# A two-layer model on one core: layer 0's experts in blocks of 256 and 128 rows

## The chip, the cores and the metric

The kernel runs on one NeuronCore of a Trainium2 chip. A core has five engines with a queue of instructions each: TensorE (PE, matrix multiplication, results into PSUM), VectorE (DVE), ScalarE (ACT), GpSimd (POOL) and SyncE (SP). DMAs are issued from the queues of SP, ACT and POOL. The metric is the time of one execution in microseconds of device time, the median of several runs. Numbers are float32 throughout, apart from one mask.

## The reference

Two layers work on 32 sequences of 256 tokens with 128 channels, so on T = 8192 tokens. Each layer computes `x = x + s * silu(f)`, where `s` is an attention over the normalized tokens and `f` a mixture of experts over the same tokens:

```
xn = layernorm(x)
s = attention(xn)          # layer 0: causal, (q1 k1 / 8) (q2 k2 / 8) v; layer 1: strided softmax
scores = sigmoid(xn @ gate_w + bias)         # layer 0
top_scores, top_idx = top_k(scores, 2)       # 2 of 8 experts a token
top_scores = top_scores / (sum(top_scores) + 1e-6)
eo = gelu(xn @ up_w[e] + up_b[e]) @ down_w[e] + down_b[e]     # 128 -> 512 -> 128
out = shared(xn) * 0.1 + sum over the two experts of 0.1 * top_score * eo
out = out / (max(abs(out)) + 1e-6)
x = x + s * silu(out)
```

The reference sends each token through all eight experts of layer 0 and weighs the results, of which two count. No token is dropped there, so an expert may have any number of rows, and the sum over the experts is 2T = 16,384 rows. In layer 1 each expert has a capacity of 2048 rows.

## The kernel before, in words

The kernel is written with Tile, a layer that orders the instructions of each engine at compile time, by the order in the program and by when their inputs are ready in its own model, and that sets the semaphores. Instructions put through `inline` keep their order among themselves on their engine.

Layer 0 goes through these stages:

1. `begin` normalizes the tokens and computes the gates' logits. Two steps of attention run beside each part.
2. `route0` (L626) picks two experts for each token, counts, and works out for each of the 16,384 (token, expert) rows its place (`slot0`) in a buffer in DRAM, `disp0`. The rows of an expert lie together and fill whole blocks of TB = 256 rows; the last block of an expert is partly empty. With sizes known only at run time, NB = (2T + 8 x 255) // 256 = 71 blocks are always worked on, whatever the counts. Positions come from matmuls with triangular matrices into two PSUM tiles (`pos`). From the counts (`psn`) a chain of small VectorE instructions makes the number of blocks of each expert (`nb`), their running sum (`ends`), the base of each expert (`base`), the place of each row (`own`, then `slot`), and for each block the rows of the weight table that it needs (`ex0`, then `wrow`). The function yields in between, and three steps of attention are issued at each yield (`RS = 3`).
3. `dispatch` (L697) scatters the 16,384 rows into `disp0`, 128 at a time, in 128 indirect DMAs of POOL. `pace` (L143) sends three and then waits for their landing. A step of attention runs beside four of every five.
4. `experts` (L914) takes the blocks one after the other. `fetch` (L902) gathers the weights of block i + 2 from DRAM into one of three buffers (`wt`, an indirect DMA of POOL, 592 KB), and loads the block's rows (`xd`, from SP). A block is transposed on PE (`xdt`, copied to `xdT` by DVE), multiplied with the up weights (`eup`, two PSUM tiles of 512 columns, so two 128-channel parts of the 512 in each), put through Gelu by ACT into `ha`, and, one block later, multiplied with the down weights (`edn`). DVE adds the bias (`od`), ACT multiplies each row with its gate, and POOL scatters 128 rows at a time to their tokens in `moe0`, at indices (`to`, by `places`, L180) that POOL works out from the row's own number.
5. The rest of the steps of attention run beside `combine0`, which adds up, normalizes and finishes layer 0. Layer 1 follows.

The attention of layer 0 is a generator of 256 steps (`attention0`, 8 for each of 32 sequences). `step` (L1033) issues the next one, with a piece of the shared expert. The main program hands the steps out: 30 beside `begin`, 12 in routing (four yields), 103 in dispatch, 71 beside the experts. `experts` yields after the transposes, after each half of the up-projection and after the down-projection, four times a block, and a step is issued at every fourth yield (`BLOCK = 4`). That makes 216; 40 are left for the combining stage, whose plan counts from there.

What sets the order around the change: PE works through its queue in the compiled order, so a block whose weights have not landed holds up everything behind it. The three `wt` buffers mean that the gather of block i + 2 can start when block i - 1 is done. On POOL the gathers share a queue with the scatters and with `to`, whose four buffers make it wait for earlier scatters. The three PSUM tiles of `mm_tile` are shared by all these stages.

Of the kernel before, what the change touches and what calls it, by code (L numbers as in the profile page):

```python
# [57 lines left out]
def model_kernel(ctx: ExitStack, tc: tile.TileContext, a: dict, out: bass.AP):  # L58
# [17 lines left out]

    NB = (2 * T + E * (TB - 1)) // TB
    disp0 = dram.tile([(2 * T // TB + E) * TB, ROW], F32, name="disp0")
# [205 lines left out]
    def mm_tile(name):  # L284
        return ps_m.tile([P, 512], F32, tag="mm", name=name)
# [256 lines left out]
    with ExitStack() as c0:  # L542
# [83 lines left out]
        def route0():  # L626

            with ExitStack() as cr:
# [7 lines left out]
                NJ = T // TB  # L636
                starts = rp.tile([P, NJ], F32, name="starts")
                nc.gpsimd.iota(starts, [[TB, NJ]], base=0, channel_multiplier=0,
                               allow_small_or_imprecise_dtypes=True)
                more = rp.tile([P, E, NJ], F32, name="more")  # L640
                nc.vector.tensor_tensor(more, bc(psn[:, :E], 2, NJ), bc(starts, 1, E), ALU.is_gt)
                nb = rp.tile([P, E], F32, name="nb")
                nc.vector.tensor_reduce(nb, more, AX.X, ALU.add)
                ends = nb
                for d in (1, 2, 4):
                    e2 = rp.tile([P, E], F32, name=f"ends{d}")
                    nc.vector.tensor_copy(e2[:, :d], ends[:, :d])
                    nc.vector.tensor_tensor(e2[:, d:], ends[:, d:], ends[:, : E - d], ALU.add)
                    ends = e2
                base = rp.tile([P, E], F32, name="base")  # L650
                nc.vector.tensor_tensor(base, ends, nb, ALU.subtract)
                nc.vector.tensor_scalar(base, base, float(TB), -1.0, ALU.mult, ALU.add)
                own = rp.tile([P, E, 2 * NT], F32, tag="totb", name="own")
                for e in range(E):
                    nc.vector.scalar_tensor_tensor(own[:, e, :], pos[e // 4][:, e % 4, : 2 * NT],
                                                   base[:, e : e + 1], ohf[:, e, :], ALU.add, ALU.mult)
                slot = rp.tile([P, 2 * NT], F32, name="slot")
# [4 lines left out]

                blk = rp.tile([P, NB], F32, name="blk")
                nc.gpsimd.iota(blk, [[1, NB]], base=0, channel_multiplier=0,
                               allow_small_or_imprecise_dtypes=True)
                row = rp.tile([P, 1], F32, name="row")
                nc.gpsimd.iota(row, [[0, 1]], base=0, channel_multiplier=1,
                               allow_small_or_imprecise_dtypes=True)
                ex0 = rp.tile([P, NB], F32, name="ex0")
                nc.vector.tensor_scalar(ex0, blk, ends[:, 0:1], None, ALU.is_ge)  # L670
                for e in range(1, E - 1):
                    nc.vector.scalar_tensor_tensor(ex0, blk, ends[:, e : e + 1], ex0, ALU.is_ge, ALU.add)
                nc.vector.tensor_scalar(ex0, ex0, float(P), row, ALU.mult, ALU.add)
# [24 lines left out]
        def dispatch():  # L698
            for k in range(2):
                if k:  # L700
                    nc.gpsimd.tensor_scalar(xr[:, :, P], xr[:, :, P], float(-T), None, ALU.add)
                    nc.gpsimd.tensor_copy(xr[:, :, P + 1], gate0[:, 1, :])
                for n in range(NT):
                    out0.put(slot0[:, k, n : n + 1], xr[:, n, :], NB * TB)
                    yield
# [144 lines left out]
        def attention0():  # L850
# [48 lines left out]
            for _ in tail:  # L899
                pass  # L900

        def fetch(i):  # L902

            wt = ek.tile([P, NW], F32, tag="wt", name="wt", bufs=3)
            nc.gpsimd.indirect_dma_start(
                out=wt, out_offset=None, in_=a["wexp"][:, :],
                in_offset=bass.IndirectOffsetOnAxis(ap=wrow[:, i : i + 1], axis=0),
            )
            xd = ek.tile([P, TB // P, ROW], F32, tag="xd", name="xd", bufs=4)
            get = nc.sync.dma_start(xd, disp0[i * TB : (i + 1) * TB, :].rearrange("(p s) d -> p s d", p=P))  # L910
            out0.behind(get)
            return wt, xd

        def experts():  # L914

            got = {i: fetch(i) for i in range(2)}
            last = None
            for i in range(NB + 1):
                if i < NB:
                    if i + 2 < NB:  # L920
                        got[i + 2] = fetch(i + 2)
                    wt, xd = got.pop(i)
                    pst = mm_tile("xdt")
                    with queued([PE] if i == 0 else []):
                        for s in range(TB // P):
                            nc.tensor.transpose(pst[:, s * P : (s + 1) * P], xd[:, s, :P], ident)
                    xdT = ek.tile([P, TB], F32, tag="xdT", name="xdT")
                    nc.vector.tensor_copy(xdT, pst[:, :TB])
                    yield
                    ha = ek.tile([P, NFC, TB], F32, tag="ha", name="ha", bufs=2)  # L930
                    for h in range(2):
                        psu = mm_tile("eup")
                        for f in (2 * h, 2 * h + 1):
                            pu = psu[:, (f % 2) * TB : (f % 2 + 1) * TB]
                            nc.tensor.matmul(pu, lhsT=wt[:, f * P : (f + 1) * P], rhs=xdT,  # L935
                                             start=True, stop=True)
                        for f in (2 * h, 2 * h + 1):
                            pu = psu[:, (f % 2) * TB : (f % 2 + 1) * TB]
                            b = FF + NFC * P + f
                            nc.scalar.activation(ha[:, f, :], pu, AF.Gelu, bias=wt[:, b : b + 1])  # L940
                        yield
                if last is not None:
                    wl, hl, xl = last
                    tl = places(ek, xl)
                    psd = mm_tile("edn")[:, :TB].rearrange("p (s c) -> p s c", s=TB // P)
                    for s in range(TB // P):
                        for f in range(NFC):
                            nc.tensor.matmul(psd[:, s, :], lhsT=hl[:, f, s * P : (s + 1) * P],  # L948
                                             rhs=wl[:, FF + f * P : FF + (f + 1) * P],
                                             start=(f == 0), stop=(f == NFC - 1))  # L950
                    od = ek.tile([P, TB // P, P], F32, tag="od", name="od")
                    nc.vector.tensor_tensor(od, psd, bc(wl[:, NW - P : NW], 1, TB // P), ALU.add)
                    for s in range(TB // P):
                        nc.scalar.activation(od[:, s, :], od[:, s, :], AF.Copy, scale=xl[:, s, P + 1 : P + 2])  # L954
                        back0.put(tl[:, s : s + 1], od[:, s, :], 2 * T, order=at_once)
# [129 lines left out]
        for n, _ in enumerate(experts()):  # L1085
            if n % BLOCK == 0:
                step()
# [272 lines left out]
```

## Time and profile before

| what | us |
|---|---|
| time, median of 3 runs | 1929.27 (1926.44 to 1931.02) |
| the profiled execution: its own time | 1932.48 |
| its span, first to last instruction | 1930.6 |
| PE busy (matmuls) | 1805.7, 94% of the span |
| DVE, ACT, POOL busy | 1175.4, 962.0, 847.5 |
| routing, 142 to 190 | 48: PE busy 46.8, DVE 46.2 |
| dispatch, 190 to 452 | 262: PE busy 258.3, DVE 181.0, POOL 137.7 |
| experts, 452 to 938 | 486: PE busy 472.8, ACT 232.7, POOL 226.7, DVE 184.0 |
| combining, 938 to 1153 | 215: PE busy 179.7, DVE 161.5 |
| layer 1, from 1153 | 778 |

Times are counted from the first instruction of the profiled execution. Busy time is the union of an engine's instructions. PEld is the loading of weights into the array, which lies beside the matmuls. One matmul of float32 shows as two records. In a line of the timeline the columns are start, length, engine, line of the kernel, operation, what is written and read, and the number of instructions merged into the line; in square brackets is how long the engine was idle before it, and what ended the wait. In a line of a group the columns behind the bars are the busy time, the mean length of one record in ns, and the idle time before them with what ended it.

### The profile page before, as it was taken

What the parts mean: (1) busy time and instruction counts of PE and PEld (TensorE: products, weight loads), DVE (VectorE), ACT (ScalarE), POOL (GpSimd) and SP (SyncE); (2) the same over time, 40 slices, a digit from 0 to 9 for tenths busy, and PEclk for the clock granted to TensorE, in tenths of its full rate; (3) what the DMA queues carried; (4) which work ended last, traced back from release to release, by engine and by line L of the source; (5) the groups of instructions that cost most, each with busy time, mean ns of one, the idle gap of its engine ahead of it and who ended that gap; (6) DMA issues with size and microseconds to landing.
All of it is one profiled execution on the core that took longest, in us unless ns stands there. A gap on an engine that the chain in (4) does not pass through costs nothing.

```text
span 1930.6 us, 45909 instructions
## 1 busy us (share of the span) xinstructions
PE 1805.7 (94%) x18616; PEld 1394.5 (72%) x18616; DVE 1175.4 (61%) x2227; ACT 962.0 (50%) x2180; POOL 847.5 (44%) x991
## 2 busy tenths in 40 slices
PE   5999999998999999999887799999999799999997
PEld 4777777776888888887765676677777577777765
DVE  6659667665333433443577597888888433335786
ACT  5433333334444544545354575577677333335776
POOL 3001555543444544444545540044544355555454
PEclk8999999999999999999988777999999899999998
DMA  8911211112344443434334410211111122222343
GB/s 279 385 52 31 69 56 43 45 44 67 126 137 125 138 142 125 134 125 137 116 105 143 137 50 7 71 67 34 32 34 33 51 73 67 72 69 84 90 113 101
DMA packets 127524, 183.86 MB, mean 95 GB/s; under 512 B 16340, under 2 KB 83183, under 8 KB 127312
## 3 DMA queue, kind: packets, MB, share of 16 engines
q1 hardware_dynamic: 96096, 92.45, 16.2%
q0 software_dynamic: 28336, 79.73, 12.3%
q10 hardware_dynamic: 2880, 8.74, 1.2%
q8 instruction: 147, 2.41, 0.5%
q14 instruction: 65, 0.53, 0.1%
HBM read 104.11 MB, written 78.00 MB: 94 GB/s over the span
## 4 chain that ended last, share of the span: by engine, by line
PE 31%; ACT 8%; DVE 5%; DMA 2%; issue 2%; POOL 2%; SPq 1%; ACTq 0%; DVEq 0%; POOLq 0%
PE mpsu L1186 6%; PE mpsd L1200 6%; PE apsc L378 3%; PE apsT L406 3%; PE apav L415 3%; ACT apT L408 3%; ACT apr L398 2%; PE apsk L338 2%; PE apsc L384 2%; DMA rows<-moe 1%; PE apsq L350 1%; PE apsv L358 1%; PE mpst L1179 1%; DVE apr L396 1%; DMA soin<-part 1%
## 5 line engine op out<-in xcount | busy, mean ns | idle before, releaser
L166 POOL DMA_INDIRECT moe<-od,to x270 | 270.0, 1000 | 124.3 <-issue 70.8
L777 ACT COPY qk<-ptr 128x512 f32<-128x512 f32 x256 | 138.2, 588 | 241.9 <-PE ptr L775 241.4
L792 DVE TENSOR_TENSOR pat<-pp,dmask 128x1024 f32<-128x1024 f32 x128 | 156.2, 1221 | 109.6 <-PE pp L790 109.6
L395 DVE TENSOR_REDUCE amx<-apsc 128x4 f32<-128x496 f32 x256 | 170.2, 665 | 38.6 <-PE apsc L384 38.5
L408 ACT COPY apT<-apsT 124x512 f32<-124x512 f32 x256 | 142.8, 584 | 100.8 <-PE apsT L406 99.9
L790 PE MATMUL pp<-qk 64*128 64x128 f32 x2048 | 172.6, 297 | 15.8 <-DVE pat L792 14.1
L790 PEld LDWEIGHTS pp<-qk 64*128 64x128 f32 x2048 | 136.8, 194 | 58.4 <-issue 42.5
L396 DVE TENSOR_TENSOR apr<-apsc,amx 128x496 f32<-128x496 f32 x256 | 172.4, 673 | 9.1
L940 ACT ACTIVATE ha<-eup,wt 128x256 f32<-128x256 f32 x284 | 119.0, 471 | 111.8 <-PE eup L935 57.7
L935 PE MATMUL eup<-xdT,wt 128*128 128x256 f32 x568 | 150.2, 390 | 10.8 <-ACT od L954 7.1
L166 POOL DMA_INDIRECT disp<-xr,slot x128 | 132.4, 1034 | 62.7 <-issue 26.7
L744 DVE TENSOR_TENSOR feat<-rot 128x1024 f32<-128x1024 f32 x128 | 157.5, 1272 | 3.9
L406 PE MATMUL apsT<-ident,apr 128*124 128x128 f32 x1024 | 150.7, 293 | 8.3 <-ACT apr L398 3.5
L775 PE MATMUL ptr<-ident,feat 128*128 128x128 f32 x1024 | 146.9, 288 | 7.6 <-DVE feat L744 7.6
L166 POOL DMA_INDIRECT disp<-xr,sidx x128 | 126.7, 990 | 55.0 <-issue 24.7
L415 PE MATMUL apav<-ava,apT 124*64 124x9 f32 x4096 | 143.4, 205 | 0.0
L415 PEld LDWEIGHTS apav<-ava,apT 124*64 124x64 f32 x4096 | 136.8, 140 | 8.8 <-issue 8.4
L948 PEld LDWEIGHTS edn<-wt,ha 128*128 128x128 f32 x1136 | 137.8, 192 | 3.6
L948 PE MATMUL edn<-wt,ha 128*128 128x128 f32 x1136 | 138.1, 275 | 0.0
L775 PEld LDWEIGHTS ptr<-ident,feat 128*128 128x128 f32 x1024 | 114.7, 145 | 29.9 <-issue 13.9
L406 PEld LDWEIGHTS apsT<-ident,apr 128*124 128x124 f32 x1024 | 120.9, 148 | 16.2 <-ACT apr L398 8.8
L935 PEld LDWEIGHTS eup<-xdT,wt 128*128 128x128 f32 x568 | 99.5, 190 | 45.0 <-issue 27.4
(250 smaller groups left out, 3342.8 us busy)
## 6 DMA issues: line engine op xcount, KB each, us to landing
disp<-zero SPq DMA_DIRECT2D x17, 1040.0 KB, 8.5
rows<-moe SPq DMA_DIRECT2D x64, 256.0 KB, 3.9
xd<-disp SPq DMA_DIRECT2D x71, 130.0 KB, 2.3
xd<-disp SPq DMA_DIRECT2D x32, 260.0 KB, 2.8
x<-in_x SPq DMA_DIRECT2D x32, 256.0 KB, 4.6
moe<-zero SPq DMA_DIRECT2D x8, 1024.0 KB, 14.4
part<-so ACTq DMA_DIRECT2D x16, 512.0 KB, 3.5
soin<-part SPq DMA_DIRECT2D x16, 512.0 KB, 4.7
```

The costliest lines, as they stand in the source:

```text
L166: ins = order(lambda: nc.gpsimd.indirect_dma_start(out=self.dst[:, :], out_offset=bass.IndirectOffsetOnAxis(ap=idx, axis=0), in_=rows, in_ ...
L395: inline(nc.vector.tensor_reduce(mx, sv, AX.X, ALU.max))
L396: inline(nc.vector.tensor_tensor(to, sv, bc(mx, 2, NK), ALU.subtract))
L406: nc.tensor.transpose(psT[:NK, j, :], pr[:, 4 * g + j, :], ident)
L408: inline(nc.scalar.copy(pT[:NK], psT[:NK]))
L415: nc.tensor.matmul(avv[u * QB : (u + 1) * QB, h, :], lhsT=pT[:NK, j, u * QB : (u + 1) * QB], rhs=va[:NK, 2 * st + u, h, :], start=True, st ...
L744: inline(eng.tensor_tensor(f[:, n].rearrange("p (h i j) -> p h i j", i=D, j=D), bc(r[:, n], 3, D), bc(r[:, 2 + n], 2, D), ALU.mult))
L775: inline(nc.tensor.transpose(pst[:, 2 * n + c], seq.feat[c][:, n, m * P : (m + 1) * P], ident))
L790: inline(nc.tensor.matmul(pp[:, w, i, c], lhsT=qk[r, 2 + c], rhs=qk[r, c], start=True, stop=True))
L792: inline(nc.vector.tensor_tensor(pat.rearrange("p w i c q -> p (w i c) q"), pp.rearrange("p w i c q -> p (w i c) q"), bc(dmask, 1, 8), ALU ...
L935: nc.tensor.matmul(pu, lhsT=wt[:, f * P : (f + 1) * P], rhs=xdT, start=True, stop=True)
L948: nc.tensor.matmul(psd[:, s, :], lhsT=hl[:, f, s * P : (s + 1) * P], rhs=wl[:, FF + f * P : FF + (f + 1) * P], start=(f == 0), stop=(f == ...
```

## The change

Layer 0's blocks get two sizes. Of each expert's rows, as many blocks of 256 are taken as can be filled with more than 128 rows in the last one; a rest of 1 to 128 rows gets a block of 128. All the blocks of 256 lie first in `disp0`, the small ones behind. There are always 60 places of 256 rows and 15 of 128 (units of 128 rows: 135, where it were 142); where the experts need more than 60 whole blocks, the others are worked on as two small ones each. The blocks are taken in turns: four of 256, then one of 128.

- `route0` counts for both sizes: tiles of twice the width, `shift` and `full` for the rows that go to small blocks, two instructions for each expert on `own` where it was one, and one product over all of it. The table of the blocks' experts takes 15 instructions on `ex0` where it took 7.
- `route0` yields once more, in the middle of `own`, so three more steps of attention are issued in routing.
- A small block has one transpose, one PSUM tile of 4 x 128 columns for the up-projection, Gelus of 128 columns, half the down-projection and one scatter of rows. It yields three times where a whole block yields four times: 285 yields in all.
- No step of attention is issued before the 16th yield of the experts. With one at every fourth from there, 68 steps run beside the experts where it were 71. The sum before combining stays 216.

```diff
-    NB = (2 * T + E * (TB - 1)) // TB
+    HB = TB // 2
+    WHOLE = (2 * T // HB - E) // 2
+    NU = (2 * T + E * (HB - 1)) // HB
+    NB = NU - WHOLE
...
-                starts = rp.tile([P, NJ], F32, name="starts")
+                starts = rp.tile([P, 2, NJ], F32, name="starts")
...
-                more = rp.tile([P, E, NJ], F32, name="more")
-                nc.vector.tensor_tensor(more, bc(psn[:, :E], 2, NJ), bc(starts, 1, E), ALU.is_gt)
-                nb = rp.tile([P, E], F32, name="nb")
-                nc.vector.tensor_reduce(nb, more, AX.X, ALU.add)
+                more = rp.tile([P, E, 2 * NT], F32, tag="totb", name="more")[:, :, : 2 * NJ]
+                nc.vector.tensor_tensor(more, bc(psn[:, :E], 2, 2 * NJ),
+                                        bc(starts.rearrange("p k j -> p (k j)"), 1, E), ALU.is_gt)
+                begun = rp.tile([P, E, 2], F32, name="begun")
+                nc.vector.tensor_reduce(begun, more.rearrange("p e (k j) -> p e k j", k=2), AX.X, ALU.add)
+                nb = rp.tile([P, 2, E], F32, name="nb")
+                nc.vector.tensor_copy(nb[:, 0, :], begun[:, :, 1])
+                nc.vector.tensor_tensor(nb[:, 1, :], begun[:, :, 0], begun[:, :, 1], ALU.subtract)
...
+                shift = rp.tile([P, E], F32, name="shift")
+                nc.vector.tensor_scalar(shift, ends[:, 0, :], ends[:, 0, E - 1 :], -float(TB), ALU.subtract, ALU.mult)
+                nc.vector.scalar_tensor_tensor(shift, base[:, 1, :], float(HB), shift, ALU.mult, ALU.add)
+                full = rp.tile([P, E], F32, name="full")
+                nc.vector.tensor_scalar(full, nb[:, 0, :], float(TB), None, ALU.mult)
...
                 for e in range(E):
-                    nc.vector.scalar_tensor_tensor(own[:, e, :], pos[e // 4][:, e % 4, : 2 * NT],
-                                                   base[:, e : e + 1], ohf[:, e, :], ALU.add, ALU.mult)
+                    ps = pos[e // 4][:, e % 4, : 2 * NT]
+                    nc.vector.tensor_scalar(own[:, e, :], ps, full[:, e : e + 1], shift[:, e : e + 1],
+                                            ALU.is_gt, ALU.mult)
+                    nc.vector.scalar_tensor_tensor(own[:, e, :], ps, base[:, 0, e : e + 1], own[:, e, :],
+                                                   ALU.add, ALU.add)
+                    if e == 3:
+                        yield
+                nc.vector.tensor_tensor(own, own, ohf, ALU.mult)
...
-                for e in range(1, E - 1):
-                    nc.vector.scalar_tensor_tensor(ex0, blk, ends[:, e : e + 1], ex0, ALU.is_ge, ALU.add)
+                for k in range(2):
+                    for e in range(E - 1):
+                        nc.vector.scalar_tensor_tensor(ex0, blk, edge[:, k, e : e + 1], ex0, ALU.is_ge, ALU.add)
...
+            i = turns[i]
...
+            m = TB if i < WHOLE else HB
+            r = i * TB if i < WHOLE else (WHOLE + i) * HB
+            xd = ek.tile([P, TB // P, ROW], F32, tag="xd", name="xd", bufs=4)[:, : m // P]
+            get = nc.sync.dma_start(xd, disp0[r : r + m, :].rearrange("(p s) d -> p s d", p=P))
...
+            each = WHOLE // (NB - WHOLE)
+            for i in range(NB - WHOLE):
+                turns.extend(range(each * i, each * i + each))
+                turns.append(WHOLE + i)
...
-                    for h in range(2):
+                    fs = 512 // m
+                    for h in range(NFC // fs):
...
         for n, _ in enumerate(experts()):
-            if n % BLOCK == 0:
+            if n % BLOCK == 0 and n >= 16:
                 step()
```

## The prediction

> **What bounds the kernel now.** I read the totals first, then a table of busy time by stage, then the timelines of the two stages that the change touches.
>
> ```profile
> PE 1805.7 (94%) x18616; PEld 1394.5 (72%) x18616; DVE 1175.4 (61%) x2227; ACT 962.0 (50%) x2180; POOL 847.5 (44%) x991
> ...
> 142.00:190.00 48.00, 46.77 (x532) 37.13 (x533) 46.24 (x88) 19.08 (x40) 4.59 (x6) 1.00 0.05 17
> 190.00:452.00 262.00, 258.31 (x3042) 196.43 (x3040) 180.95 (x221) 92.23 (x218) 137.68 (x170) 1.00 0.16 52
> 452.00:938.00 486.00, 472.75 (x4009) 394.83 (x4010) 184.00 (x299) 232.66 (x583) 226.71 (x279) 1.00 0.40 126
> ```
>
> The columns are the stretch, its length, and busy us of PE, PEld, DVE, ACT, POOL; then clock, DMA share, GB/s. Routing (142 to 190) fills PE and DVE alike. Dispatch (to 452) keeps PE at 99%, yet its length is set by POOL's scatters, sent three at a time. Experts (452 to 938) have PE busy 97% and nothing else above 48%: work taken from PE there is time.
>
> The costs of the experts, from the groups of that stage and from two blocks of its timeline:
>
> ```profile
> L935 PE MATMUL eup<-xdT,wt 128*128 128x256 f32 x568 | 150.2, 390 | 10.8 <-ACT od L954 7.1 <-DMA wt<-in_wexp,wrow 1.0
> L948 PE MATMUL edn<-wt,ha 128*128 128x128 f32 x1136 | 138.1, 275 | 0.0
> L926 PE MATMUL xdt<-ident,xd 128*128 128x128 f32 x142 | 27.4, 275 | 4.4 <-DMA xd<-disp 4.4
> ...
> 603.98 0.38 PE L926 MATMUL xdt<-ident,xd 128*128 128x128 f32 x2
> 605.28 1.99 PE L935 MATMUL eup<-xdT,wt 128*128 128x256 f32 x8
> 607.11 1.95 PE L948 MATMUL edn<-wt,ha 128*128 128x128 f32 x16
> ```
>
> Eight records 256 wide take 1.99 us (0.249 each), sixteen 128 wide take 1.95 (0.122 each). The group means of 275 and 390 ns are latencies that overlap, not prices.
>
> Then what a PE with less to do will run into. POOL's own row in this stage, and the wait before the first block:
>
> ```profile
> 454.46 0.66 PE L926 MATMUL xdt<-ident,xd 128*128 128x128 f32 x2 [4.44 <-DMA xd<-disp]
> ...
> 475.83 1.01 POOL L905 DMA_INDIRECT wt<-in_wexp,wrow  x1 [0.52 <-issue]
> 477.14 1.01 POOL L166 DMA_INDIRECT moe<-od,to  x1 [0.30 <-issue]
> 478.45 1.00 POOL L166 DMA_INDIRECT moe<-od,to  x1 [0.30 <-ACT qk L777]
> 481.03 0.19 POOL L184 TENSOR_SCALAR to<-xd 128x2 int32<-128x2 f32 x1 [1.58 <-DMA moe<-od,to]
> 481.99 1.00 POOL L905 DMA_INDIRECT wt<-in_wexp,wrow  x1 [0.77 <-DVE od L952]
> ```
>
> This is a ring: gather, two scatters, their landing, the next index row `to`, the next gather. Here it takes 6.16 us; a whole block takes 481.6/71 = 6.78. With other landings (last scatter to `to`: 2.43 to 3.95 us, about 3.0 in the twelve I read) it is 1.31 + 1.31 + 3.0 + 0.19 + 0.5 = 6.3. So POOL, 47% busy, is 7% from setting the pace. Last, DVE in routing:
>
> ```profile
> 175.51 0.42 DVE L641 TENSOR_TENSOR more<-psn,starts 128x256 f32<-128x256 f32 x1 [0.95 <-PE psn L635]
> 177.99 2.15 DVE L655 SCALAR_TENSOR_TENSOR own<-gpos,base,gohs 128x128 f32<-128x128 f32 x8
> 180.06 1.21 DVE L792 TENSOR_TENSOR pat<-pp,dmask 128x1024 f32<-128x1024 f32 x1
> 181.19 1.95 DVE L658 TENSOR_REDUCE slot<-own 128x128 f32<-128x1024 f32 x1
> 183.25 0.22 DVE L659 CAST slot<-slot 128x128 int32<-128x128 f32 x1
> ```
>
> From the counts to the slots it is one chain on DVE, 8 us, and no scatter starts before its end. PE meanwhile waits once, because the positions hold two of the three shared PSUM buffers until `own` has read them:
>
> ```profile
> 179.16 3.84 PE L829 MATMUL dn<-dnw,hs 128*128 128x128 f32 x32 [0.56 <-DVE own L655]
> ```
>
> **The change part by part.**
>
> Rows. 71 x 256 = 18,176 rows become 60 x 256 + 15 x 128 = 17,280: seven units of 128 less. Transposes 7 x 0.19 = 1.3 us. Down: 7 x 8 x 0.122 = 6.8. Up: 71 x 1.99 = 141.3 becomes 60 x 1.99 + 15 x 8 x 0.122 = 134.0, so 7.3. Together 15.4 us off PE. The 0.122 of a 128-wide record is the down row, same shape, with weight loads of the same 190 ns.
>
> [...] The two rows above are exactly linear, so I go by them.
>
> Routing. On DVE's chain: compare and reduction at double width, +0.26 each (0.68 for 512 elements in this stage, against 0.42); two copies +0.3; three small ones for `shift` and `full` +0.5; eight more instructions on `own` at the 0.26 pitch, +2.1; the product with `ohf` over 1024 elements +1.2. Sum 4.6 us. Three steps of attention now come in the middle; their DVE work is 180.95/103 = 1.8 us a step at most, 5.4. So slots come 4.6 to 10.0 later. I take 6.5: nearer the low end, because in the 8 us shown only one step instruction (`pat`, 1.1 us) got between, and PE's next work is the 3.8 us of `dn`, which gives DVE nothing. The ten more instructions of the block table (2.4 us on DVE, one iota more on POOL) feed gathers whose data is used 270 us later; dispatch, with DVE 69% busy, hides them.
>
> The scatters follow the slots at their own pace, so the first block also starts 6.5 later. In that time PE does the three steps: (472.75 - 150.2 - 138.1 - 27.4)/71 = 2.2 us each by the experts, 258.31/103 = 2.5 by dispatch; 7.0 for three. They leave the experts (71 steps become 68). Their copies and Gelus go to ACT, 19 of 48 us busy here, with at most one `part` store of 0.33 us on ACT's queue; SP and POOL get nothing from them. The first half of `own` now ends some 1.5 us later, so `dn` waits longer for its PSUM buffer, inside the same slack. PE's idle changes by 6.5 - 7.0 = -0.5 (bounds -2.4 and +3.4); the 4.44 us wait shown takes it.
>
> Four blocks without steps. The first copy (`xdT`, 0.4) loses its cover: 0.6. Gather 3 lands 6.1 us after block 0's down (468.5 to issue at 469.81, then the median 4.8), PE has 5.7 us of work until it needs it: 0.4. Block 4 waits for the ring, 6.3 against 4.65 of work: 1.65. Block 5: 0.1. Sum +2.8; zero at best, 5 if every ring is 7.
>
> More blocks. Four more gathers, `to` rows, copies, and loads on SP: DMA (gathers of 592 KB at a share of 0.40) and SP have room, POOL's part is in the ring; PE idles 9 us over 71 blocks now, so +0.5 to +0.8, taken 0.7. Seven scatters fewer. A small block sends one row scatter: -1.3 us behind the last block, in the chain into the combining loads; half taken, -0.7. ACT's 128-wide Gelus stay under the next block's up-projection.
>
> Late weights. The next late thing. A gather needs the block three back to be done. A small block in between takes about 1.1 us of PE work from two such spans. Landing against first up-projection today, for the 35 gathers whose landing is recorded: 11 have 0.1 to 1.0 us to spare; less 1.1, they fall short by 6.1 us in all, 0.17 a gather; times 30 spans, +5.2. Bounds 0 (the steps' shifting phase gives some spans a second step) and 16 (every second span short by 1.1).
>
> Sum: -15.4 - 0.5 + 2.8 + 0.7 - 0.7 + 5.2 = -7.9. The profiled execution took 1932.48 (span 1930.6, 1.9 around it), 0.17% above the median of 1929.27. Less 7.9 it is 1924.6; the median becomes 1921.4.
>
> **The rivals.**
>
> Nothing waits: the step phases cover the weights, start-up costs 1, slots come at 4.6. -15.4 - 2.4 + 1 + 0.7 - 0.7 = -16.8, 1912.5. For it: PE waited only 1.0 us for weights in 71 blocks. Against it: eleven slacks under 1 us.
>
> The waits eat it: late weights at 13 instead of 5.2, the rest as summed: about 1929. For it: the ring at 6.3 against 31.2/5 = 6.24 of PE work a block in a group of five.
>
> Slower, by the ring: POOL sets the pace of the whole stage. From the first gather of the ring (8.3 us in) to the end (4.8 landing, 4 of PE) there are 57 whole rings and 14 shorter by 1.3: 71r - 1.1 us against 481.6 now; with 6.5 later and 0.7 saved, it ends at 71r - 476.9. Slower by 0.2% from r = 6.77; at 6.8 it is +5.9, 1935. For it: landings up to 3.95 us make single rings of 7. Against it: 6.3 is the mean, and where `to` was queued behind the gather instead, gathers followed in 4.91 (604.93 to 609.84).
>
> **How the numbers follow.** The summed case 0.52, nothing waits 0.14, eaten 0.19, slower 0.15. Faster by over 0.2% (3.9 us, about what a measurement can tell, the runs shown spread over 0.24%): 0.52 + 0.14, less 0.03 for the summed case's upper edge, 0.63; same 0.21; slower 0.16. The range goes from just below 1912.5 to the slower case short of its tail: 1911 to 1934.
>
> **What would show it.** Right: up group near 143 us and down group near 131; first transposes of the experts near 461, last down near 929 (936 now); PE waiting for `wt` some 5 us in all (1.0 now). Wrong: 128-wide up records far from 0.122; slots later than 10 us; PE waiting over 15 us for weights; or a changed order of instructions in the combining stage, which I take as unchanged because the step count at its start is 216 in both.

## The result

The changed kernel takes 1938.8 us (median, 1929.11 to 1947.4), the kernel before 1928.76 in the same comparison (1918.52 to 1941.24). The ratio is 1.0052, with a 95% interval of 1.0035 to 1.0069: slower by about 10 us. The prediction, 1921.4 with a range of 1911 to 1934, missed both the sign and the range. The profiled execution took 1945.86 us (span 1944.1), 13.4 above the profiled execution of before; it lies 7.1 above its own median, so the two traces are further apart than the medians.

### The profile page after: what moved, and what is told of

The parts are those of the page before. It is cut to its first block, busy times and chain, and to the rows that moved or that the text cites. A ratio compares the mean times of both kernels' runs of the same rounds, so it can differ in the third digit from the quotient of the medians.

```text
span 1944.1 us, 45924 instructions
## 1 busy us (share of the span) xinstructions
PE 1789.2 (92%) x18585; PEld 1381.7 (71%) x18585; DVE 1186.2 (61%) x2259; ACT 956.2 (49%) x2189; POOL 854.5 (44%) x993
## 4 chain that ended last, share of the span: by engine, by line
PE 32%; ACT 7%; DVE 6%; DMA 2%; POOL 2%; issue 2%; SPq 0%; ACTq 0%; DVEq 0%; POOLq 0%
PE mpsu L1231 6%; PE mpsd L1245 6%; PE apsc L384 4%; PE apsT L412 3%; ACT apT L414 3%; PE apav L421 3%; ACT apr L404 2%; PE apsc L390 2%; PE apsk L344 2%; DMA rows<-moe 1%; PE apsq L356 1%; DMA soin<-part 1%; PE apsv L364 1%; DVE feat L774 1%; PE mpst L1224 1%
## 5 line engine op out<-in xcount | busy, mean ns | idle before, releaser
L172 POOL DMA_INDIRECT moe<-od,to x263 | 262.7, 999 | 122.5 <-issue 62.7
L807 ACT COPY qk<-ptr 128x512 f32<-128x512 f32 x256 | 138.1, 588 | 248.8 <-PE ptr L805 248.6
L172 POOL DMA_INDIRECT disp<-xr,slot x128 | 137.8, 1077 | 71.5 <-issue 26.7
L978 PE MATMUL eup<-xdT,wt 128*128 128x256 f32 x600 | 138.9, 372 | 26.3 <-DMA wt<-in_wexp,wrow 10.3
L997 DVE TENSOR_TENSOR od<-edn,wt 128x256 f32<-128x256 f32 (+1 forms) x75 | 29.8, 397 | 186.1 <-PE edn L993 111.7
L993 PEld LDWEIGHTS edn<-wt,ha 128*128 128x128 f32 x1080 | 131.2, 193 | 4.9 <-issue 1.4
L993 PE MATMUL edn<-wt,ha 128*128 128x128 f32 x1080 | 133.4, 276 | 0.0
```

Of the source, the lines that this page charges most:

```text
L172: ins = order(lambda: nc.gpsimd.indirect_dma_start(out=self.dst[:, :], out_offset=bass.IndirectOffsetOnAxis(ap=idx, axis=0), in_=rows, in_ ...
L978: nc.tensor.matmul(psu[:, f * m : (f + 1) * m], lhsT=wt[:, g * P : (g + 1) * P], rhs=xdT, start=True, stop=True)
```

## The profile after

First the totals and the stretch of the experts (busy us of PE, PEld, DVE, ACT and POOL, then clock, DMA share, GB/s):

```profile
PE 1789.2 (92%) x18585; PEld 1381.7 (71%) x18585; DVE 1186.2 (61%) x2259; ACT 956.2 (49%) x2189; POOL 854.5 (44%) x993
...
452.00:938.00 486.00, 448.14 (x3848) 378.02 (x3846) 179.47 (x301) 222.06 (x576) 233.11 (x286) 0.98 0.42 129
```

PE is busy 16.5 us less in the whole kernel (1805.7 before), so the work did leave. The time did not: in the stretch of the experts PE is busy 448 of 486 us, where it was 473. The groups of the experts (the first line holds the 120 records 128 wide as well as the 480 that are 256 wide):

```profile
L978 PE MATMUL eup<-xdT,wt 128*128 128x256 f32 x600 | 138.9, 372 | 26.3 <-DMA wt<-in_wexp,wrow 10.3
L993 PE MATMUL edn<-wt,ha 128*128 128x128 f32 x1080 | 133.4, 276 | 0.0
```

Against 150.2 and 138.1 before, that is 16.0 us less (predicted near 143 and 131, 14 less). These sums count the tail of the last record of each run of matmuls, which overlaps with what follows; counted from start to next start, 10.6 us fall away, transposes included (see below). And 26.3 us of idle time stand in front of the up-projection, where there were 10.8. The waits of PE (what was waited for, us in total, times, longest; `issue` is idle time for which the profile names nothing) divide them:

```profile
PE xdt L968 <- DMA xd<-disp: 11.6, 1, 11.6
PE eup L978 <- DMA wt<-in_wexp,wrow: 10.3, 12, 1.7
PE eup L978 <- issue: 5.3, 6, 1.9
PE eup L978 <- DVE xdT L970: 5.0, 7, 1.9
PE eup L978 <- ACT od L999: 3.9, 10, 1.6
```

Before, there were 4.4 us for the first `xd`, 1.0 for weights, 7.1 for ACT, and neither of the other two. The first line is a stall of its own: PE has done its steps at 459.66 and stands until 471.27, because the last scatter came late. Where the time went, point by point in the two traces:

| | before | after | difference | predicted |
|---|---|---|---|---|
| `slot` is cast | 183.25 | 189.93 | +6.7 | +6.5 |
| first scatter | 184.4 | 191.4 | +7.0 | +6.5 |
| train: first to last scatter | 265.1 | 274.8 | +9.7 | 0 |
| first expert transposes | 454.46 | 471.27 | +16.8 | +6.5 |
| stage: from there to the last down-projection | 481.6 | 478.05 | -3.5 | -13.7 |
| of it PE busy | 470.8 | 451.8 | -19.0 | -22.4 |
| of it PE idle | 10.8 | 26.3 | +15.5 | +8.7 |
| rest of the span | 994.6 | 994.8 | +0.2 | -0.7 |

(Predicted busy: the 15.4 of the rows and 7.0 of three steps; idle: 2.8, 0.7 and 5.2.) So three things were missed: the train (9.7 us), idle time in the stage (6.8) and work that was to leave PE and did not (3.4).

What lengthens the train shows in POOL's timeline, around the first three gathers of weights. After:

```profile
221.10 1.00 POOL L938 DMA_INDIRECT wt<-in_wexp,wrow  x1 [0.30 <-PE psu L852]
222.41 0.97 POOL L938 DMA_INDIRECT wt<-in_wexp,wrow  x1 [0.30 <-DMA disp<-xr,slot]
...
223.68 0.94 POOL L938 DMA_INDIRECT wt<-in_wexp,wrow  x1 [0.19 <-issue]
224.93 1.01 POOL L172 DMA_INDIRECT disp<-xr,slot  x1 [0.30 <-issue]
...
232.35 0.10 POOL L156 MEMSET breath<- 128x1 f32 x1 [3.84 <-DMA disp<-xr,slot]
```

`breath` is the wait for three scatters to land. Ordinarily it takes 1.5 us here (the median of all). Three gathers now come nearly back to back. The `breath` that falls between them (223.35) has nothing to wait for, but the next group of scatters starts only behind the third gather, and its landing takes 3.84 us. The two groups take 7.7 and 8.2 us where a group takes 5.85 in the median of before, 4.2 of the 9.7 us that the train is longer; the rest lies in other groups. In the kernel before, two gathers stood behind the first group of scatters and one behind the second, from 188 to 196:

```profile
188.46 1.00 POOL L905 DMA_INDIRECT wt<-in_wexp,wrow  x1 [0.30 <-PE psv L749]
...
190.31 1.38 POOL L905 DMA_INDIRECT wt<-in_wexp,wrow  x1 [0.61 <-issue]
...
196.32 0.98 POOL L905 DMA_INDIRECT wt<-in_wexp,wrow  x1 [0.30 <-issue]
197.47 0.10 POOL L150 MEMSET breath<- 128x1 f32 x1 [0.17 <-DMA disp<-xr,slot]
```

The table of the blocks' experts (`ex0`, `wrow`) is longer now, and the steps' DVE work stands between its instructions; `wrow` is cast at 204.6, where it was 186.3. The compiled order of POOL puts the gathers later, and all three at one place.

## The experiments

The same kernel is not equally fast on all chips. The runs with gathers moved by hand and three weight buffers, and the run without small blocks, were on a chip on which the kernel before takes 1929.11 us; all the others were on chips on which it takes 2017 to 2019. On these slower chips PE itself is late at the first transposes of the experts (no idle time before them in any of the ten traces), so there the train cannot show in the time, only in the trace. Ratios are to the kernel before on the same chip. A trace is one execution, and the executions of one kernel on one chip lie 10 to 25 us apart: lengths read from a pair of traces carry that.

**What makes the train longer.** Where no gather was moved by hand, the train takes 264 to 266 us in every trace with the old routing, and 271 to 277 in every one with the new. First the new blocks with the routing arithmetic of before. Edit: `route0` as before, so the table of blocks is worked out in 7 instructions:

```
-                nc.vector.tensor_scalar(ex0, blk, edge[:, 0, E - 1 :], 1.0 - E, ALU.is_ge, ALU.mult)
-                for k in range(2):
-                    for e in range(E - 1):
...
+                nc.vector.tensor_scalar(ex0, blk, ends[:, 0:1], None, ALU.is_ge)
```

> The changed kernel with the routing arithmetic of the kernel before (one block size, 8 instructions on own instead of 17, half as wide a table), the extra yield and the experts as changed. The rows then lie as for blocks of 256 only, so blocks are multiplied with weights of the wrong experts and the rows behind the 17,280th are dropped: only its time is read. If the longer chain on DVE is paid in full, slots come 4 to 5 us sooner than in the changed kernel, the first transposes too, and the time falls by 4 to 5 us. If PE has other work for that time, it falls by less than 2.

Measured: ratio 1.0103 (1.0063 to 1.0142); `slot` at 182.2, train 266.1. The train is that of the old routing, so routing makes it long, not the blocks. The slots come 8.9 us sooner than in a kernel with the new arithmetic on this chip (191.1, with four weight buffers), not 4 to 5. The time is none the shorter: PE is late on this chip, and idle in the stage was 34.6 us. So here the blocks lose 1% without the new routing.

Then the one thing that the traces point to, moved alone. In the kernel after, the three gathers go to three groups of their own (`n` is the turn, `pull` the gather; the dependency orders them on POOL, and the gather at 235.58 below starts 0.30 us after the scatter ahead of it, as scatters do):

```
+    NEXT = mybir.DependencyInfo(mybir.DependencyClass.NoSync, mybir.DependencyReason.DATA)
...
+            if n < 3:
+                tc.add_manual_dep(pull.ins, out0.all[(20, 38, 56)[n]].name, NEXT, reason="where it goes")
```

> The kernel after, with one thing moved: the first three weight gathers, which stand in front of one and the next of the scatters' groups (at 221 to 224 us in the traced execution), go to three groups of their own, one behind the 21st, one behind the 39th and one behind the 57th scatter. All else on every queue stays in its place. Theory B (the bunched gathers lengthen the train): the train of 128 scatters falls from the 271 to 276 us of the kernels with the new routing to 265 to 268, and the kernel is as much as 6 us shorter, less where PE is what is late at the first expert transposes. Theory V (the VectorE work that the new routing puts beside the first scatters does it): the train stays at 271 to 276.

And the reverse, in the kernel before: its gathers together behind the 18th scatter, `(17, 17, 17)` in the same line.

> The kernel before, with one thing moved: its first three weight gathers, which go one by one beside the first three groups of scatters, go behind the 18th scatter, two back to back and the third one group later, as they stand in the kernel after. Theory B: the train of scatters grows from 265 to 269 or more. Theory V: it stays within 1.5 us of 265.

Measured, on the same chip: spread in the kernel after, the train is 267.4 (274.8 in the first trace), and PE waits 3.5 us for the first block where it waited 11.6. Bunched in the kernel before, the train is 270.7 (265.1) and that wait is 10.3 (4.4). The values in brackets are those of the first two traces. Nothing else on any queue had moved. The first transposes and POOL with a gather spread, in the kernel after:

```profile
466.11 0.41 PE L971 MATMUL xdt<-ident,xd 128*128 128x128 f32 x2 [3.46 <-DMA xd<-disp]
...
235.58 1.00 POOL L939 DMA_INDIRECT wt<-in_wexp,wrow  x1 [0.30 <-PE ptr L806]
236.94 0.10 POOL L157 MEMSET breath<- 128x1 f32 x1 [0.36 <-DMA disp<-xr,slot]
```

and bunched, in the kernel before:

```profile
223.65 0.94 POOL L906 DMA_INDIRECT wt<-in_wexp,wrow  x1 [0.19 <-issue]
...
230.97 0.10 POOL L151 MEMSET breath<- 128x1 f32 x1 [2.50 <-DMA disp<-xr,slot]
```

A single gather fits into the wait for landing (0.36 us of it are left instead of 1.5); three in a row do not, and the group behind them lands late. That is theory B in both directions: 7.4 us less, 5.6 more. On the same chip the kernel without small blocks, whose gathers are bunched, has a train of 272.6; all four kernels with spread gathers have 265.8 to 267.8, the eight traces with the new routing and bunched ones 270.8 to 276.5. In the time neither effect is shown: 1.0047 (1.0016 to 1.0077) for the spread gathers is not clear of the 1.0052 of the first comparison, and 1.0021 (0.9994 to 1.0049) for the bunched ones not clear of 1. The 2.3 us by which the spread train is longer than that of before are in its first groups, beside the longer DVE work; no run takes these apart further.

**Where the stage's idle time comes from.** Three candidates: too few weight buffers, the steps, the blocks. The kernel after with a fourth buffer (`bufs=3` becomes `bufs=4` in `wt`):

> The changed kernel with four weight buffers (wt) where it has three; all else as changed. Theory W (weights): in the experts PE now outruns the gathers, because a gather must wait for the block three back; its waits for wt (10.3 us in 12 places in the profile of the changed kernel) and part of what follows them go, the stage gets 8 to 12 us shorter than 478, and the time comes down by as much, to about that of the kernel before. Theory D (dispatch): what was lost lies before the experts, in the later and longer train of scatters (first transposes 16.8 us later); the stage is then bound by the steps and copies all the same, and the time changes by less than 3 us.

Measured: 1.0062 (1.0035 to 1.0089). PE no longer waits for weights at all, but is still idle 26.2 us in the stage: the waits are put down to `issue` (8.6), ACT (`od` 5.1, `vz` 3.2), `xdT` (4.3) instead. The wait for weights stood in front of others. The kernel after itself was not run on this chip, so the ratio does not say what the buffer gives.

The kernel after with the steps handed out as before (no yield inside `own`, 71 in the experts), and the kernel before with only the steps moved:

```
-                    if e == 3:
-                        yield
...
-            if n % BLOCK == 0 and n >= 16:
+            if n % BLOCK == 0 and n >= 4:
```

> The changed kernel with the steps of attention handed out as before: no yield inside own, so 12 steps in routing, and from the 4th yield of the experts on one at every fourth, 71 in all. Theory W: the stalls for weights stay (the first blocks have steps again, so some 3 us of them go); seven us of steps come back into the experts; slots come about 5 us later than in the kernel before instead of 6.7, and PE waits for them; time about 5 us above the kernel before. Theory D: with fewer steps mixed into routing the train starts at most 5 us later and the experts' saving of 15 us shows: 5 to 10 us below the kernel before.

> The kernel before with the steps of attention handed out as in the change: a yield inside own (15 steps in routing), none before the 12th yield of the experts (68 steps there); all blocks have 256 rows. Theory W: the first blocks run without steps and wait for their weights, 2 to 4 us, the later ones as before; slots 2 us later; time 0 to 4 us above the kernel before. Theory D: the steps in the middle of routing push the slots and the train back by most of the 6.7 us and cost 4 to 8 us.

Measured: the blocks with their routing 1.0101 (1.0059 to 1.0142), stage 494.7, idle 30.0; the steps alone 1.0014 (0.9991 to 1.0038), stage 477.5, idle 15.1, train 264.4. So the moved steps are free within what can be told, and the loss belongs to the blocks and their routing. It is some 20 us on this chip; for the blocks theory W had 5 and theory D a gain, and both were wrong.

A whole block yields four times and a small one three times, so the step at every fourth yield moves to another place in the block after each small one. In the kernel after the same 68 steps, tied to the place behind the first half of the up-projection, beside a run of the kernel after on the same chip:

```
-                        yield
+                        yield h == 0 and i >= 4 and (m == TB or turns[i] >= WHOLE + 3)
...
-        for n, _ in enumerate(experts()):
-            if n % BLOCK == 0 and n >= 16:
+        for here in experts():
+            if here:
```

> The changed kernel once more, as the mark for the runs beside it and for a second profile. Ratio to the kernel before 1.005 as in the first comparison. If the longer train of scatters (274.8 us in the first profile against 265.1) comes from the new routing, it is 270 to 275 again; if it was that execution's own, it is 264 to 267.

> The changed kernel, but the 68 steps beside the experts are tied to the blocks: none in the first four, then one behind the first half of the up-projection of each whole block and behind the up-projection of 12 of the 15 small ones, where the change issues one at every fourth yield and so at a place in the block that moves on by one with every small block. Theory P (phase): the moving place lets the copies of xdT stand behind the step's work on DVE and ACT; PE's waits for them (5.0 us named xdT, 5.3 us without a name, 1 us named tu, of 26.3 idle in the stage) go, and the time falls by 5 to 10 us against the changed kernel. Theory W (weights): the idle time of PE moves to waits for wt and the time stays within 3 us.

Measured: 1.0094 (1.0072 to 1.0116) for the kernel after, 1.0046 (1.0026 to 1.0066) with the steps tied: 10 us of 19 are back. The train of the kernel after is 274.6 again, so it was not that first execution's own. In the stage, PE waits for `xdT` 0.2 us where it was 7.4, and is idle 25.6 where it was 33.5; first the kernel after, then with the steps tied:

```profile
PE eup L978 <- DVE xdT L970: 7.4, 9, 2.1
...
PE eup L978 <- DVE xdT L970: 0.2, 1, 0.2
```

The copy `xdT` is a DVE instruction of 0.42 us; where a step comes just ahead of it, the step's work is in front of it on DVE. One such place in the kernel after, DVE first and then PE:

```profile
537.69 2.36 DVE L774 TENSOR_TENSOR feat<-rot 128x1024 f32<-128x1024 f32 x2
539.97 0.42 DVE L970 COPY xdT<-xdt 128x256 f32<-128x256 f32 x1
...
540.44 2.15 PE L978 MATMUL eup<-xdT,wt 128*128 128x256 f32 x6 [1.89 <-DVE xdT L970]
```

The transposes are done at 537.97, the copy starts 2.0 us later behind two `feat`, and PE stands for 1.89.

With the fourth buffer on top, and with the gathers spread on top:

> The kernel of f2 with four weight buffers. If P and W both hold and add up, PE's idle time in the experts falls from 26 us to about 12, as in the kernel before (10.8), and the time is 12 to 15 us below the changed kernel, so some 3 us below the kernel before. If POOL's queue itself is the limit (theory of the ring: gather, scatters, landing, index row), a fourth buffer gives nothing beyond f2.

> The kernel after with the steps tied to one place in the block, and the first three gathers spread over three groups of scatters. Theory B: the train is 265 to 268 instead of 271.5; with that the ratio to the kernel before, 1.0046 for the steps tied alone, falls to 1.002 to 1.004, and below 1 only if the scatters and not PE are late at the first expert transposes. Theory V: train 271 to 276, ratio 1.0046 again.

Measured: the fourth buffer gives 1.0061 (1.0041 to 1.0081), against 1.0046 without it on the same chip: nothing in the time. In the traces the stage is 8.0 us shorter (481.0 and 473.0) and PE's idle time 20.7 instead of 25.6, but the one traced execution lies 6.7 us above its median and the other 10.2 below, so this pair settles nothing. Tied steps and spread gathers give 1.0018 (0.9992 to 1.0044), train 265.8, stage 476.2: no longer measurably slower than before, nor faster. PE's idle time is 20.7. Its waits, in the stage:

```profile
PE eup L981 <- DMA wt<-in_wexp,wrow: 10.7, 11, 1.9
PE eup L981 <- ACT od L1002: 6.8, 20, 0.7
PE eup L981 <- issue: 0.7, 1, 0.7
PE eup L981 <- DVE xdT L973: 0.2, 1, 0.2
```

`xdT` and `issue` are gone, ACT is where it was before the change (7.1), and the weights remain. All three together:

> The kernel after with the steps tied to a place in the block, the first gathers spread over groups of scatters of their own, and four weight buffers where it were three. If the 10.7 us of waiting for weights that the kernel with spread gathers and tied steps still has are a cost of their own, the experts' stage falls from 476.2 to 466 to 469 and the ratio to the kernel before from 1.0018 to 0.996 to 0.998: this version would be faster than both. If they only stand in front of the next wait (ACT, which frees the PSUM tiles of the up-projection), idle time in the stage goes from 20.7 to 16 or more with the waits of the up-projection for ACT at 10 or more, and the ratio stays within 1.000 to 1.003.

Measured, on a chip where PE is late at the first block: 1.0058 (1.004 to 1.0077), idle 20.6.

```profile
PE eup L981 <- ACT od L1002: 10.1, 19, 2.5
PE eup L981 <- issue: 3.5, 6, 1.7
```

The 11 us of waiting for weights are gone and the idle time is the same as in the stage with three buffers (20.7, on the other chip): 3.3 us more are put down to ACT, 2.8 more to `issue`, the rest to smaller waits of other matmuls. That is the second of the two outcomes expected in the trace; the ratio, though, is above the 1.000 to 1.003 that went with it. The train counts for nothing on this chip, which would raise it; no run tests that.

**What a small block costs.** The kernel with tied steps, without the work on small blocks:

```
-                turns.append(WHOLE + i)
...
+            NB = WHOLE
```

> This kernel leaves out the work on the 15 small blocks: no weights, no products, their rows of the dispatch buffer are put into the result as they are, behind the last whole block; its total time is not comparable, the stage from the first expert transposes to the last down-projection is. It has the 60 whole blocks, and the 68 steps tied to places. Prices as predicted: a small block is 0.19 + 0.98 + 0.98 = 2.15 us of PE, so the stage is 15 x 2.15 = 32 us shorter than that of the same kernel with small blocks (481.0, 473.0 with four weight buffers), if the small blocks cost nothing beyond their products: about 449. Theory F (a block has a fixed price whatever its size, some 0.6 us): 15 x 2.8 to 3.5 = 42 to 52 us shorter, 430 to 439, and PE's own time in the expert instructions, start to next start, 41 us or more below 277.

Measured: stage 430.6, PE idle 10.0, waits for weights 2.0. The stage here, and that of the tied steps and spread gathers (length, then busy us as above):

```profile
468.95:899.57 430.62, 420.64 (x3614) 347.48 (x3614) 167.50 (x266) 202.10 (x504) 195.88 (x241) 1.00 0.39 121
...
464.86:941.06 476.20, 455.46 (x3871) 382.61 (x3871) 174.49 (x296) 225.14 (x580) 224.92 (x279) 0.99 0.42 131
```

Against 476.2 with the small blocks (tied steps, spread gathers, same chip), 15 small blocks cost 45.6 us, 3.04 each: theory F's stage. PE's own time in the expert instructions (start to next start, without idle time) is 240.0 against 271.1, so 31.1 for the small ones, 2.07 each: the predicted price (2.15), and not theory F's 41 (the 277 of the expectation is 271.1 by this count). The other 14.5 us are idle time (20.7 against 10.0, of which weights 10.7 against 2.0) and 3.8 that show in no idle record and lie in the steps between. Theory F was right in the stage and wrong in the reason: what comes on top of the products is mostly waiting.

A whole block takes 240.0 / 60 = 4.00 us of PE's own time. Its price in the stage is less certain: the kernel before (bunched gathers, same chip) has a stage of 482.1 with 71 of them and three more steps, 51.5 us more. With 2.2 for a step and the 2.8 reckoned for four blocks without steps, both from the prediction, that is 47.7 for eleven, 4.34 each; with the 2.67 that a step takes from start to next start (189.9 us for 71) and without the 2.8, 43.5, 3.95 each. So fifteen small blocks (45.6) cost the stage about what the eleven whole ones did that they replace (43.5 to 47.7): there was nothing to win in the stage.

**Filling what is left.** Four steps more beside the scatters and four fewer in the experts, on the version with tied steps and four buffers; and one step, on the version with all three:

```
-            if n % 5 != 4:
+            if n % 5 != 4 or n < 20:
```

> The kernel of f3 with four more steps in dispatch and four fewer beside the experts. Theory D (dispatch): PE waits 11.6 us for the first block because the train of scatters ends 17 us later than before; four steps, some 9 us, fit into that wait, the first block starts no later, the experts get 9 us less of PE work, and the time falls by another 6 to 9 us. If the experts are then held by POOL or by the copies, or if PE has no such wait here, it falls by less than 3.

> The same with one step of attention more beside the scatters and one less beside the experts. Where the scatters are late at the first expert transposes (PE idle there 3.4 us in the kernel with spread gathers and tied steps), the step fills idle time: 2.2 us off the stage and at most 0.5 added before it, ratio 0.001 below that of the run beside it. Where PE is late there (as on the chips on which the kernel before takes 2018 us), it is moved and nothing is won.

Measured: 1.0123 (1.0092 to 1.0153) and 1.0086 (1.006 to 1.0111), both worse than without. On these chips PE has no idle time before the first block, so the steps make it later: the first transposes are at 491.8 against 477.6 with four steps, at 485.5 against 477.1 with one. That is more than the steps' own 2.67 us each, and the stage did not win in return (476.7 against 473.0, 481.5 against 477.6); both stay unexplained. No version tried beats the kernel before.

## Why the prediction was wrong

At the last down-projection the prediction had 7.2 us less and the trace has 13.3 more. Of these 20.5 us, 10.3 arise before the first block and 10.2 in the stage: 6.8 of idle time and 3.4 of work. These are two traces; between the medians it is 10.0 us more where 7.9 less were forecast.

- **"The scatters follow the slots at their own pace"** is the step that failed first: +9.7 us in the train. The ten more instructions of the block table were costed at nothing, because the gathers' data is used 270 us later. That is true of the data and not of the queue: the gathers stand between scatters that are paced by their landing, and with the later table they moved from the first two pauses (two and one) to one place (three). The prediction named dispatch as set by POOL's scatters and did not ask what else is in that queue. Spreading them takes back 7.4 us of the train, bunching them in the old kernel costs 5.6. With the old routing the gathers stay early (187 to 194) and the train short; that it is the table in it, and not the rest, is read from `wrow` and was not tested alone.
- **Routing, 6.5 later** (bounds 4.6 to 10): 6.7 in the first trace. The mechanism was right, the number in part luck:

```profile
173.75 0.69 DVE L647 TENSOR_TENSOR more<-psn,starts 128x512 f32<-128x512 f32 x1 [0.95 <-PE psn L641]
...
183.18 1.29 DVE L762 TENSOR_TENSOR tu<-psp,cs 128x512 f32<-128x512 f32 x2 [0.19 <-PE psp L757]
...
185.17 1.21 DVE L822 TENSOR_TENSOR pat<-pp,dmask 128x1024 f32<-128x1024 f32 x1
...
189.93 0.22 DVE L682 CAST slot<-slot 128x128 int32<-128x128 f32 x1
```

  From the counts (`more`) to the slots it is 16.2 us where it was 7.7, so 8.4 more: 4.8 of its own instructions (predicted 4.6) and 3.6 of step instructions between them, `tu` and `pat` above among them (predicted 1.9). In this trace the counts came 1.8 us earlier than before; in the pair on the chip of the moved gathers, 183.40 and 191.36, the slots are 8.0 later.
- **Rows, -15.4** is the step that failed in the work: the experts' matmuls, counted from start to next start without idle time, take 281.1 us before and 270.5 after, 10.6 less (10 to 11 on the chip of the moved gathers: 281.2 against 269.8 and 271.1). The prediction priced a block by the lengths of its rows, 0.38 + 1.99 + 1.95 = 4.32, and each length holds the tail of its last record, over which the next instruction already runs: `eup` at 605.28 is followed at 607.11, `edn` at 607.11 by

```profile
608.89 0.38 PE L926 MATMUL xdt<-ident,xd 128*128 128x128 f32 x2
```

  So they take 1.83 and 1.78, and a whole block 281.1 / 71 = 3.96. In the same way a step took 2.67, not 2.2, so the three steps moved out gave 8.3 us instead of 7.0. The price of the small block's up-projection is right: eight records start at 945.48, and the next instruction at 946.47, 0.99 us later (0.124 each).

```profile
945.48 1.16 PE L978 MATMUL eup<-xdT,wt 128*128 128x128 f32 x8
946.47 2.84 PE L993 MATMUL edn<-wt,ha 128*128 128x128 f32 x24
```

  By the same count 0.124 is 0.54 of the 0.229 (1.83 / 8) of a 256-wide record, near the half that was assumed, so going by the two rows was right here. By the run without small blocks, one takes 2.07 us of PE's own time, as priced; it was the whole blocks taken away that were priced too high. What comes on top of the work is waiting, by the next two points.
- **Late weights, +5.2** (0 to 16). The mechanism and the place were right: of the 12 waits after, 11 are at the first or second whole block behind a small one, 8.7 us in all, where there were 1.0 before, at two blocks; the twelfth, 1.66, is block 3, one of the blocks without steps. So +7.7 against 5.2, a term undersized by 2.5.
- **The moving place of the steps** was in the prediction only as a help (a bound of 0 for late weights). It is a cost: waits for `xdT` of 5.0 us and 5.3 of `issue`, both new, while the waits for ACT fell by 3.2. Tying the steps takes 5.9 us off the stage in one pair (486.9 to 481.0) and 2.3 in the other (478.5 to 476.2); in the time it is 1.0094 against 1.0046.
- **Three steps moved, four blocks without steps, one scatter fewer.** The first two are at no measurable loss (1.0014, 0.9991 to 1.0038). The -0.7 at the end did not appear (+0.2).
- **The rival that ended slower**, POOL's ring setting the pace of the whole stage at 1935, is near in time and not the cause. Its condition, rings of 6.77 us throughout, would show as a wait at nearly every block; there are 12 in 75.

Why the kernel after loses more on the chip of its second run (1.0094) than on the first (1.0052) is open: idle in the stage is 33.5 there against 26.3, and it was not taken apart.

## What to carry to other kernels

Here a queue was paced by landings, and one gather fitted into a pause where three in a row cost the train 5.6 to 7.4 us: look in such a queue for what else stands in it. When an edit makes the input of such a transfer later, read where the compiled order puts it next, however late its data is needed. Two streams interleaved by counting keep their phase only while all items have equal counts (waits for `xdT` of 7.4 us by the count, 0.2 tied), so tie the one to a place in the other before items become unequal. Price an instruction from its start to the next one's start, not by its length (1.83 against 1.99 us for a whole block's `eup`). And price a smaller item by taking it away, with the waits behind it: half the rows took half of PE's work (2.07 against 4.00 us), and 3.04 us of time against a whole block's 4.0 to 4.3.

## What the runs showed of the hardware

- The same kernel takes 1929 us on one chip and 2017 to 2019 on three others, 4.6% more; what is hidden differs with it. On the slower ones PE does not wait before the first block in any of ten traces, and the train is off the path.
- After the wait of 11.6 us the granted clock was 0.50 from 462.8 to 476.4; before, with a wait of 4.4, from 454.4 to 457.8 (mean over 450 to 480: 0.77 and 0.94). PE had stopped at 459.66 and 450.02, so half speed was granted 3.1 and 4.4 us into the pauses. Sixteen `pp` records took 2.08 us at 0.50 (from 471.86) and 1.16 at 1.00 (from 453.96). Of the 13.6 us at half, 5.1 were under work, against 3.3 before: some 0.9 us more lost, as an estimate (half of the difference).
- A fourth weight buffer removes every wait for weights (10 to 11 us, gone in all five kernels that had it) and no measurable time. The same matmuls then wait more for ACT or without a name (with tied steps `od` 7.5 and then 11.4 us, `issue` 2.1 and then 3.6); how much of the 11 us comes back so differs from pair to pair.
